# Raw features first for layer 0 of a bidirectional minGRU, with a late token scale and its chunks put between fusion tiles

## The chip, the cores and the metric

One NeuronCore of a Trainium2 chip runs the whole program. The metric is the device time of one execution in microseconds (us). TensorE is called PE, its weight loads PEld, VectorE DVE, ScalarE ACT, GpSimd POOL, SyncE SP.

## The reference

The input x is 8 batches of 512 tokens with 512 features. It is normalised per token, goes through four gated recurrent layers once forward and once backward in time with the same weights, both directions are joined by a linear layer ("fusion") and added to x. A feed-forward part with ternary weights follows; the change does not touch it.

```python
def mingru(x, W, b):                       # Wz = Wh = W, bz = bh = b in this case
    z  = sigmoid(x @ W.T + b)
    ht = tanh(x @ W.T + b)
    a  = clip(1.0 - z, 1e-8, 1 - 1e-8)
    return linear_scan(a, z * ht)          # h[t] = a[t]*h[t-1] + z[t]*ht[t]
def stack(x):
    h = x
    for i in range(4):
        h_new = mingru(h, W[i], b[i]) + (h if i > 0 else 0)
        h = layernorm(h_new, gamma, beta)  # per token, over 512 features
    return h
xn  = (x - mean(x)) / sqrt(var(x) + 1e-5)  # per token, without gamma and beta
x   = x + concat(stack(xn), flip(stack(flip(xn)))) @ fusion_W.T + fusion_b
out = x + ffn(layernorm_plain(x))          # absmean ternary weights, gelu, layernorm
```

## The kernel before

Everything is fp32. A **state** is one batch in one direction, kept features first: a tile `h` of 4 chunks of 128 features by 512 tokens (pool `h`, 6 buffers). Batches go in four pairs. Layers 1 to 3 run over the four states of a pair; layer 0 gives both directions of a batch from one set of gates, because it has the same input for both.

**The order is written out by hand** (`manual_schedule`). Its unit is a **slot** (function `slot`): some main work, and shares taken from queues. The main work of a layer is one **gate** chunk (`gates`, L378): four matmuls, which PE records as 8 passes, into a PSUM tile `u` (pool `ps_u`, 3 buffers), three activations on ACT (the factors a, z, t, L385 to L387), on DVE the clamp of a (L390) and the product z = z*t (L391), then the time scan (L400) and the residual add. Layer 0 does two scans for a chunk, one for each direction.

After a layer its state is normalised by going to tokens and back. **T** (`tokens` on `turned`, L272): four transposes into a PSUM tile `pt` (pool `ps_t`, 3 buffers), on DVE the statistics (`bn_stats` L137, `bn_aggr`, add of eps L141), POOL's power L144 for 1/sqrt, on DVE the bias `nmr` (L259), and ACT writes the normalised token tile (L263). **B** (`back`, L281): four transposes of the four token tiles into `pf`, and ACT copies them to `h` with gamma and beta (L287). Each state has four T and four B; `turns` and `backs` queue them, a slot takes one of each, or two of each where it is called with caps of 2. The last layer needs only 1/sqrt of the variance for each token (`norm_last`), which scales the output of fusion, and its residual adds come as four in a row (L433). `need` runs slots without main work until a state is ready: an **empty slot**. `Tokens` lets a B start one slot after the last T; at most `TOK` = 12 token tiles are held at once.

**x** of a later pair is normalised in layer 3 of the pair before, by the queues `xturns` and `xbacks`: tokens are loaded (`xn`), statistics and token tile as in T but without transposes, then B as `pf_x` into `xT` (`norm_x`). For the first two batches `start_x` does it ahead of all slots.

**Fusion** (`fusion`) has four tiles a batch, of 128 tokens each: on DVE the bias `fb` is added to the loaded x row `xf` (L449), PE makes 8 passes for each direction into a tile `pu` of its own (L454, from `ps_u` as well), DVE scales each by its 1/sqrt and adds it to the row (L464), which frees the `pu`; the row is stored. Between pairs four stages follow each other: layer 0 of batch b+2, fusion of b, layer 0 of b+3, fusion of b+1. In the fusion weights `fw` gamma, beta and the mean over features are folded once: `fold_beta` (16 passes, L530, and 8 scalings by gamma on DVE) and `fold_mean` for each direction (8 passes, L547, and 4 corrections on DVE).

Two side tasks ride on every second or fourth slot (`extra`): sums of absolute ternary weights in the first pair and their quantisation in the later ones, each loaded through the pool `stg` of 4 buffers. In the last pair the first feed-forward input is normalised as well (`norm_y`). All loads but the very first go through SP's queue.

Of the kernel before, what the change touches and what calls it, by code (L numbers as in the profile page):

```python
# [24 lines left out]
def kernel(  # L25
    ctx: ExitStack,
    tc: tile.TileContext,
    x: bass.AP,
    gru_wT: bass.AP,
# [19 lines left out]

    nc = tc.nc  # L50
# [8 lines left out]
    TOK = 12  # L59
# [9 lines left out]
    zp = ctx.enter_context(tc.tile_pool(name="z", bufs=16))  # L69
# [5 lines left out]
    stgp = rec.enter_context(tc.tile_pool(name="stg", bufs=4))  # L75
# [15 lines left out]
    def load_x(use, b, t, queue):  # L91
        xs[use, b, t] = xsp.tile([P, H], F32, tag="xs", name=f"x{use}_{b}_{t}")
        queue.dma_start(out=xs[use, b, t], in_=x[b, ts(t, P), :])

    def load_gw(l, queue):
        queue.dma_start(out=gw[l], in_=gru_wT[l].rearrange("(c p) h -> p c h", p=P))
# [8 lines left out]

    warm = const.tile([P, 1], F32, name="warm")
    nc.vector.memset(warm, 0.0)
    for t in range(0, NT, 2):
        load_x("n", 0, t, nc.sync)
        load_x("n", 0, t + 1, nc.scalar)  # L110
    load_gw(0, nc.scalar)
    nc.sync.dma_start(out=gb, in_=gru_b)
    for t in range(NT):
        load_x("n", 1, t, nc.sync)
# [5 lines left out]
    for l in range(1, L):  # L120
        load_gw(l, nc.sync)
# [66 lines left out]
    ctx.enter_context(tc.manual_schedule())  # L188
    with rec:
        gp = rec.enter_context(tc.tile_pool(name="gate", bufs=3))  # L190
        ps_u = rec.enter_context(tc.tile_pool(name="ps_u", bufs=3, space=PSUM))
        ps_t = rec.enter_context(tc.tile_pool(name="ps_t", bufs=3, space=PSUM))
# [6 lines left out]
        xT = {}  # L199
# [5 lines left out]
        class Tokens(list):  # L205


            def append(self, tile_):
                super().append(tile_)
                self.at = now[0] + 1  # L210
# [6 lines left out]
        def shares(cap_t, cap_b):  # L217


            mid, last = [], []  # L220
            for q, cap in ((turns, cap_t), (backs, cap_b)):
                for _ in range(cap):
                    if not q or not ready(q[0][0]):
                        break
                    take(q, mid, last)
            return mid, last

# [40 lines left out]
        def turned(zs, t, name):  # L268
            def source():
                pt = ps_t.tile([P, H], F32, tag="pt", name=f"pt_{name}")  # L270
                for c in range(NC_):
                    nc.tensor.transpose(pt[:, ts(c, P)], zs[c][:, ts(t, P)], ident)  # L272
                return pt
# [22 lines left out]
        def norm(s, zs, tag):  # L296
# [8 lines left out]
            for t in range(NT):  # L305
                queue(turns, s, at + 2, tokens(turned(zs, t, f"{tag}_{t}"), toks, None, f"{tag}_{t}"))
# [9 lines left out]
        def norm_x(b, at, gap):  # L316
            toks = Tokens()

            def dst():
                if b not in xT:  # L320
                    xT[b] = hp.tile([P, NC_, S], F32, tag="h", name=f"xT_{b}")
                return xT[b]

            for t in range(NT):
                queue(xturns, b, at + gap * t, tokens(lambda t=t: xs["n", b, t], toks, None, f"x{b}_{t}"))
            for c in range(NC_):
                queue(xbacks, b, toks, back(toks, dst, c, False, f"x{b}_{c}"))

        def norm_y(b):
            toks = Tokens()  # L330

# [25 lines left out]

        def slot(work=None, cap_t=1, cap_b=1):
            end = work() if work is not None else None
            mid, last = shares(cap_t, cap_b)  # L360
            m, e = x_shares()
            if end is not None:
                end(mid + m)
            else:
                for f in mid + m:
                    f()
# [6 lines left out]
        def gates(h, l, o, name, scans):  # L373

            def work():
# [7 lines left out]
                t = gp.tile([P, S], F32, tag="t", name=f"t_{name}")  # L383
                a = gp.tile([P, S], F32, tag="a", name=f"a_{name}")
                nc.scalar.activation(a, u, AF.Sigmoid, bias=ngb[:, l, o : o + 1], scale=-1.0)  # L385
                nc.scalar.activation(z, u, AF.Sigmoid, bias=gb[:, l, o : o + 1])  # L386
                nc.scalar.activation(t, u, AF.Tanh, bias=gb[:, l, o : o + 1])  # L387

                def end(mid):
                    nc.vector.tensor_scalar(a, a, CLAMP_HI, CLAMP_LO, ALU.min, ALU.max)  # L390
                    nc.vector.tensor_tensor(z, z, t, ALU.mult)  # L391
# [5 lines left out]

        def scan(dst, a, z, backward):
# [3 lines left out]
        def first_layer(b, cap=1):  # L402

            need(b)
            zf, zb = [], []
            h = xT[b]
            for o in range(NC_):
                def scans(a, z, o=o):
                    f = zp.tile([P, S], F32, tag="z", name=f"zf_{b}_{o}")
                    scan(f, a, z, False)  # L410
                    scan(z, a, z, True)
                    zf.append(f)
                    zb.append(z)
                slot(gates(h, 0, o, f"{b}_0_{o}", scans), cap, cap)
            state[b, 0] = xT.pop(b)
            now[0] -= 1
            norm((b, 0), zf, f"{b}0_0")
            norm((b, 1), zb, f"{b}1_0")
            now[0] += 1

        def layer(s, l, cap=1):
            need(s)
            zs = []
            h = state[s]
            for o in range(NC_):
                def scans(a, z, o=o):
# [4 lines left out]
                    elif o == NC_ - 1:  # L431
                        for c in range(NC_):
# [9 lines left out]
        def fusion(b):  # L442
            need((b, 0), (b, 1))
            hs = [state.pop((b, 0)), state.pop((b, 1))]
            rs = [rsv.pop((b, 0)), rsv.pop((b, 1))]
            for t in range(NT):
                def work(t=t):
                    xt = xs["f", b, t]
                    nc.vector.tensor_tensor(xt, xt, fb, ALU.add)  # L449
# [10 lines left out]
                    def end(mid):  # L460
                        for f in mid:
                            f()
                        for d in range(2):
                            nc.vector.scalar_tensor_tensor(  # L464
                                xt, pus[d], rs[d][:, t : t + 1], xt, ALU.mult, ALU.add
                            )
                        nc.sync.dma_start(out=x1[b][t], in_=xt)
                    return end
                slot(work, 2, 2)
# [56 lines left out]
        def fold_beta():  # L526
            pb = ps_u.tile([P, H], F32, tag="u", name="pb")
            for k in range(2 * NC_):
                c = k % NC_
                nc.tensor.matmul(  # L530
                    pb, lhsT=bet[:, c : c + 1].broadcast_to([P, P]), rhs=fw[:, k, :],
                    start=(k == 0), stop=(k == 2 * NC_ - 1),
                )

            def end(mid):
                for f in mid:
                    f()
                nc.vector.tensor_tensor(fb, pb, fb, ALU.add)
                for k in range(2 * NC_):
                    c = k % NC_  # L540
                    nc.vector.tensor_scalar(fw[:, k, :], fw[:, k, :], gam[:, c : c + 1], None, ALU.mult)
            return end

        def fold_mean(d):
            pm = ps_u.tile([P, H], F32, tag="u", name=f"pm_{d}")
            for c in range(NC_):
                nc.tensor.matmul(  # L547
                    pm, lhsT=ones, rhs=fw[:, d * NC_ + c, :], start=(c == 0), stop=(c == NC_ - 1),
                )

            def end(mid):
                for f in mid:
                    f()
                for c in range(NC_):
                    w = fw[:, d * NC_ + c, :]
                    nc.vector.scalar_tensor_tensor(w, pm, -1.0 / H, w, ALU.mult, ALU.add)
# [3 lines left out]
        def load_pair(use, b):  # L560
            for t in range(NT):
                load_x(use, b, t, nc.sync)

        def start_x(b):

            srcs = [xs["n", b, t] for t in range(NT)]
            found = [stats([s], f"x{b}_{t}") for t, s in enumerate(srcs)]
            toks = Tokens()
            for t in range(NT):
# [296 lines left out]
```

## Time and profile before

| what | value |
|---|---|
| median of 3 runs | 1796.99 us (1794.94 to 1797.65) |
| the profiled execution | 1797.87 us, of it span 1796.1 us |
| granted PE clock, mean | 0.994 |
| PE busy | 1727.9 us (96%) |
| DVE busy | 1438.8 us (80%) |
| ACT busy | 1025.8 us (57%) |
| POOL busy | 201.9 us (11%) |
| DMA | 83.33 MB, mean 46 GB/s |

Busy is the time in which an engine works on an instruction; passes of PE are pipelined, so their sum is more than the distance from start to start, which is used for prices. The span runs from the first to the last instruction of the profiled execution. Names such as L378 are lines of the kernel before.

### The profile page before, as it was taken

Reading aid. Unit: us, or ns where it says so; the run is one execution under the profiler, and the core shown is the slowest. Engines: PE = TensorE matmul, PEld = TensorE weight load, DVE = VectorE, ACT = ScalarE, POOL = GpSimd, SP = SyncE. Lnnn points to the kernel's source line nnn. Section 1 sums busy time; section 2 is a strip of 40 time slices with the busy share of each in tenths; the row PEclk is TensorE's granted clock in tenths of the full one; section 3 lists DMA queues with packets and bytes.
Section 4 is the critical chain, followed back from the end, with each engine's and each line's share of the span. In section 5 each row is a group of like instructions: output and inputs, shape, how many; then the busy total and the mean of one; then the engine's idle time right before and its main releaser. Section 6 shows DMA issues by size and latency. Waiting matters only on the chain.

```text
span 1796.1 us, 19346 instructions
## 1 busy us (share of the span) xinstructions
PE 1727.9 (96%) x6520; PEld 1052.0 (59%) x6520; DVE 1438.8 (80%) x2863; ACT 1025.8 (57%) x1664; POOL 201.9 (11%) x334
## 2 busy tenths in 40 slices
PE   5999999999999999999999999999999999999998
PEld 2555554444555444555544455554488888888886
DVE  5888989658998966999897699988368787768776
ACT  4677776337776522677752367773055656565563
POOL 1111112100111110111111011111000000000000
PEclk9999999999999999999999999999999999999999
DMA  6002111110110121111011121001301011101100
GB/s 217 7 24 63 49 31 46 47 46 1 48 59 24 47 70 36 36 60 52 31 47 65 41 83 53 1 24 53 127 32 48 10 38 47 48 1 47 48 24 24
DMA packets 42132, 83.33 MB, mean 46 GB/s; under 512 B 5040, under 2 KB 5040, under 8 KB 41008
## 3 DMA queue, kind: packets, MB, share of 16 engines
q1 hardware_dynamic: 41216, 80.52, 13.1%
q10 hardware_dynamic: 816, 1.57, 0.3%
q8 instruction: 51, 0.84, 0.2%
q14 instruction: 49, 0.40, 0.1%
HBM read 56.91 MB, written 25.17 MB: 46 GB/s over the span
## 4 chain that ended last, share of the span: by engine, by line
PE 59%; DVE 21%; ACT 12%; issue 5%; DMA 2%; POOL 1%; DVEq 0%; SPq 0%; POOLq 0%; ACTq 0%
PE u L378 20%; PE ph L690 11%; PE po L717 11%; PE pu L454 9%; DVE z L391 4%; DVE z L400 4%; DVE st L137 3%; PE pt L272 3%; ACT tok L263 3%; PE pf L281 2%; ACT t L387 2%; ACT z L386 2%; ACT a L385 2%; ACT xT L287 1%; DVE a L390 1%
## 5 line engine op out<-in xcount | busy, mean ns | idle before, releaser
L378 PE MATMUL u<-xT,gw 128*128 128x512 f32 x1024 | 461.0, 593 | 1.6 <-ACT xT L287 1.6
L378 PE MATMUL u<-h,gw 128*128 128x512 f32 x768 | 350.2, 599 | 0.0
L263 ACT ACTIVATE tok<-pt,nmr,rs 128x512 f32<-128x512 f32 x192 | 148.3, 777 | 324.8 <-DVE nmr L259 297.6
L378 PEld LDWEIGHTS u<-xT,gw 128*128 128x128 f32 x1024 | 185.4, 191 | 186.1 <-issue 182.4
L400 DVE TENSOR_TENSOR_SCAN z<-a,z 128x512 f32<-128x512 f32 x224 | 274.0, 1223 | 2.6
L137 DVE BATCH_NORM_STATS2 st<-pt 128x6 f32<-128x512 f32 x256 | 176.6, 690 | 85.9 <-PE pt L272 85.4
L378 PEld LDWEIGHTS u<-h,gw 128*128 128x128 f32 x768 | 140.9, 193 | 140.8 <-issue 140.8
L385 ACT ACTIVATE a<-u,ngb 128x512 f32<-128x512 f32 x224 | 153.3, 684 | 107.3 <-PE u L378 104.7
L694 ACT ACTIVATE g<-ph 128x512 f32<-128x512 f32 x128 | 76.2, 595 | 229.0 <-PE ph L690 229.0
L144 POOL TENSOR_TENSOR rs<-ve,mhalf 128x1 f32<-128x1 f32 x192 | 112.7, 587 | 814.5 <-DVE ve L141 670.2
L717 PE MATMUL po<-pwq,ghi 128*128 128x512 f32 x512 | 203.5, 397 | 0.0
L690 PE MATMUL ph<-yhi,fcq 128*128 128x512 f32 x512 | 199.7, 390 | 0.0
L717 PE MATMUL po<-pwq,glo 128*128 128x512 f32 x512 | 199.6, 390 | 0.0
L690 PE MATMUL ph<-ylo,fcq 128*128 128x512 f32 x512 | 199.4, 389 | 0.0
L391 DVE TENSOR_TENSOR z<-z,t 128x512 f32<-128x512 f32 x224 | 154.2, 689 | 27.3 <-ACT t L387 24.8
L387 ACT ACTIVATE t<-u,gb 128x512 f32<-128x512 f32 x224 | 155.6, 694 | 0.0
L386 ACT ACTIVATE z<-u,gb 128x512 f32<-128x512 f32 x224 | 153.7, 686 | 0.0
L705 DVE TENSOR_TENSOR acc<-acc,g 128x512 f32<-128x512 f32 x112 | 77.2, 689 | 92.9 <-ACT g L694 91.9
L281 PE MATMUL pf<-ident,tok 128*128 128x128 f32 x768 | 116.6, 275 | 12.4 <-ACT tok L263 9.2
L454 PE MATMUL pu<-fw,h 128*128 128x512 f32 x256 | 119.9, 612 | 8.5 <-DVE xf L464 8.4
L272 PEld LDWEIGHTS pt<-ident,z 128*128 128x128 f32 x640 | 79.3, 141 | 79.4 <-issue 71.4
L454 PE MATMUL pu<-fw,xT 128*128 128x512 f32 x256 | 115.1, 592 | 0.0
(127 smaller groups left out, 2291.5 us busy)
## 6 DMA issues: line engine op xcount, KB each, us to landing
xf<-in_x_dram SPq DMA_DIRECT2D x32, 256.0 KB, 3.8
x<-xf SPq DMA_DIRECT2D x32, 256.0 KB, 2.0
xy<-x SPq DMA_DIRECT2D x32, 256.0 KB, 4.3
out_dram<-xy SPq DMA_DIRECT2D x32, 256.0 KB, 2.1
xn<-in_x_dram SPq DMA_DIRECT2D x30, 256.0 KB, 4.5
fca<-in_fc_wT_dram SPq DMA_DIRECT2D x16, 256.0 KB, 2.9
pwa<-in_proj_wT_dram SPq DMA_DIRECT2D x16, 256.0 KB, 2.7
fcb<-in_fc_wT_dram SPq DMA_DIRECT2D x16, 256.0 KB, 3.5
```

The costliest lines, as they stand in the source:

```text
L137: nc.vector.bn_stats(st[:, i, :], p)
L263: nc.scalar.activation(tile_, src, AF.Identity, bias=nmr, scale=r)
L281: nc.tensor.transpose(pf[:, ts(t, P)], toks[t][:, ts(c, P)], ident)
L378: nc.tensor.matmul(u, lhsT=gw[l][:, c, ts(o, P)], rhs=h[:, c, :], start=(c == 0), stop=(c == NC_ - 1),)
L385: nc.scalar.activation(a, u, AF.Sigmoid, bias=ngb[:, l, o : o + 1], scale=-1.0)
L386: nc.scalar.activation(z, u, AF.Sigmoid, bias=gb[:, l, o : o + 1])
L387: nc.scalar.activation(t, u, AF.Tanh, bias=gb[:, l, o : o + 1])
L391: nc.vector.tensor_tensor(z, z, t, ALU.mult)
L400: nc.vector.tensor_tensor_scan(dst[:, d], a[:, d], z[:, d], 0.0, ALU.mult, ALU.add)
L454: nc.tensor.matmul(pu, lhsT=hs[d][:, c, ts(t, P)], rhs=fw[:, d * NC_ + c, :], start=(c == 0), stop=(c == NC_ - 1),)
L690: nc.tensor.matmul(ph, lhsT=w, rhs=ys[b][c][i], start=(c == 0 and i == 0), stop=(c == NC_ - 1 and i == 1),)
L717: nc.tensor.matmul(po[b][t], lhsT=part[:, ts(t, P)], rhs=pwq[k // NP_][:, k % NP_, :], start=(k == 0 and i == 0), stop=(k == NF - 1 and i ...
```

## The change

* The program gets x a second time, as `xt`, features first; the host lays it out, as it does the weights. A batch is loaded from it as `xT` (1 MB) by `load_xT`: both batches of the first pair at the start, each later one in layer 2 of the pair before.
* At the start the column mean of the first layer's weights `gw[0]` is taken out of them, so that gates on raw x equal gates on x minus its token mean. x in tokens is still loaded, for 1/sqrt of its variance alone (`norm_x`); `scale_x` spreads that over 128 partitions by four transposes of a broadcast column and ACT copies it to a tile `scale`. Token tiles and `pf_x` transposes of x are gone.
* A chunk of layer 0 has three stages, kept in `stages`: 8 PE passes; "factors", a given number of slots later: u times `scale` on DVE, then the three activations; "scans", one slot after that. `slot` runs what is due with `due`.
* Layer 0 chunks and fusion tiles alternate. `zlive` counts the z tiles in use, and a chunk waits in empty slots if two more don't fit in 16.
* The order of the activations becomes a, t, z. The pool `ps_u` has 4 buffers (was 3), `ps_t` 2 (was 3), `stg` 3 (was 4), `t` 2 (was 3); `TOK` is 10. `norm_y` starts its B two slots after the last T.
* Folding: `fold_sums` computes the sums with beta and with gamma together, in rows 0 and 64 of one product, kept in two token tiles until layer 1; `fold` picks the gamma row, divided by 512, and corrects and scales `fw` in one DVE step a chunk; `fold_bias` picks the beta row.
* The first loads alternate between SP and ACT in chunks of 256 KB.

The diff, cut; functions that go away whole are seen in the listing above.

```diff
-    TOK = 12
+    ZT = 16
+    TOK = 10
...
+    def load_xT(b):
+        xT[b] = hp.tile([P, NC_, S], F32, tag="h", name=f"xT_{b}")
+        nc.sync.dma_start(out=xT[b], in_=xt[b].rearrange("(c p) s -> p c s", p=P))
...
-    for t in range(0, NT, 2):
-        load_x("n", 0, t, nc.sync)
-        load_x("n", 0, t + 1, nc.scalar)
-    load_gw(0, nc.scalar)
+    xT[0] = hp.tile([P, NC_, S], F32, tag="h", name="xT_0")
+    for dst, part in ((gw[0], gru_wT[0]), (xT[0], xt[0])):
+        for c in range(NC_):
+            queue = nc.scalar if c % 2 else nc.sync
+            queue.dma_start(out=dst[:, c, :], in_=part[ts(c, P), :])
+    for t in range(NT):
+        load_x("n", 0, t)
     nc.sync.dma_start(out=gb, in_=gru_b)
+    load_xT(1)
...
-        ps_u = rec.enter_context(tc.tile_pool(name="ps_u", bufs=3, space=PSUM))
-        ps_t = rec.enter_context(tc.tile_pool(name="ps_t", bufs=3, space=PSUM))
+        ps_u = rec.enter_context(tc.tile_pool(name="ps_u", bufs=4, space=PSUM))
+        ps_t = rec.enter_context(tc.tile_pool(name="ps_t", bufs=2, space=PSUM))
...
+        def scale_x(b):
+            def go():
+                pf = ps_f.tile([P, S], F32, tag="pf", name=f"pr_{b}")
+                for t in range(NT):
+                    nc.tensor.transpose(pf[:, ts(t, P)], rx[b][:, t : t + 1].broadcast_to([P, P]), ident)
+                def last():
+                    scale[b] = gp.tile([P, S], F32, tag="scale", bufs=2, name=f"scale_{b}")
+                    nc.scalar.copy(scale[b], pf)
+                return None, last
+            return go
+        def norm_x(b, at):
+            rx[b] = small.tile([P, NT], F32, tag="rsv", name=f"rx_{b}")
             for t in range(NT):
+                queue(xturns, ("x", b), at + t, tokens(lambda t=t: xs["n", b, t], None, rx[b][:, t : t + 1], f"x{b}_{t}"))
+            queue(xbacks, ("x", b), at + NT + 1, scale_x(b))
...
         def slot(work=None, cap_t=1, cap_b=1):
             end = work() if work is not None else None
+            due("factors")
             mid, last = shares(cap_t, cap_b)
             m, e = x_shares()
+            mid += m
+            late = [s for s in stages if s[0] <= now[0] and s[1] == "scans"]
+            if late or end is None:
+                for f in mid:
+                    f()
+                mid = []
+            due("scans")
             if end is not None:
-                end(mid + m)
+                end(mid)
...
+        def first_layer(b, lag=0):
...
+            def chunk(o):
+                def work():
+                    while zlive[0] + 2 > ZT:
+                        slot(None, 2, 2)
+                    zlive[0] += 2
...
+                    def scaled():
+                        z = zp.tile([P, S], F32, tag="z", name=f"z_{name}")
+                        nc.vector.tensor_tensor(z, u, scale[b], ALU.mult)
+                        a, t = factors(z, z, 0, o, name)
+                        def scans():
+                            product(a, z, t)
...
+                            scan(f, a, z, False)
+                            scan(z, a, z, True)
...
+                        stages.append((now[0] + 1, "scans", scans))
+                    stages.append((now[0] + lag, "factors", scaled))
+                return work
+            return [chunk(o) for o in range(NC_)]
         def layer(s, l, cap=1):
+            while s not in state or any(x[1] == "scans" for x in stages):
+                slot(None, 2, 2)
             need(s)
...
+        def fold_sums(d):
+            ps = ps_u.tile([P, H], F32, tag="u", name=f"pfold_{d}")
+            for c in range(NC_):
                 nc.tensor.matmul(
+                    ps, lhsT=both[:, c, :, :].rearrange("p i r -> p (i r)"), rhs=fw[:, d * NC_ + c, :],
...
+        def fold(d):
+            pm = ps_u.tile([P, H], F32, tag="u", name=f"pm_{d}")
+            nc.tensor.matmul(pm, lhsT=picks[1], rhs=folded[d], start=True, stop=True)
...
-                    nc.vector.scalar_tensor_tensor(w, pm, -1.0 / H, w, ALU.mult, ALU.add)
+                    nc.vector.scalar_tensor_tensor(w, w, gam[:, c : c + 1], pm, ALU.mult, ALU.subtract)
...
+        pm0 = ps_u.tile([P, H], F32, tag="u", name="pm0")
+        for c in range(NC_):
+            nc.tensor.matmul(pm0, lhsT=ones, rhs=gw[0][:, c, :], start=(c == 0), stop=(c == NC_ - 1))
+        for c in range(NC_):
+            w = gw[0][:, c, :]
+            nc.vector.scalar_tensor_tensor(w, pm0, -1.0 / H, w, ALU.mult, ALU.add)
+        for b in range(2):
+            norm_x(b, 0)
...
+        f0, f1 = first_layer(0, NC_ - 1), first_layer(1, 2)
+        for work in f0:
+            slot(work, 2, 2)
...
+        slot(f1[0], 2, 2)
+        slot(f1[1], 2, 2)
+        slot(lambda: fold_sums(0), 2, 2)
+        slot(f1[2], 2, 2)
+        slot(f1[3], 2, 2)
+        slot(lambda: fold_sums(1), 2, 2)
...
+            for i in range(2):
+                load_pair("f", b + i)
+                firsts = first_layer(b + 2 + i) if not last_pair else [None] * NT
+                for first, tile_ in zip(firsts, fusion(b + i)):
+                    if first is not None:
+                        slot(first)
+                    slot(tile_, 2, 2)
```

## The prediction, made before the result was known

> **What bounds the kernel now.** I read the busy table first, then the chain that ended last, then a table by stage, then the timeline of TensorE (PE) with its gaps, then VectorE (DVE) beside it.
>
> ```profile
> PE 1727.9 (96%) x6520; PEld 1052.0 (59%) x6520; DVE 1438.8 (80%) x2863; ACT 1025.8 (57%) x1664; POOL 201.9 (11%) x334
> ...
> PE 59%; DVE 21%; ACT 12%; issue 5%; DMA 2%; POOL 1%; DVEq 0%; SPq 0%; POOLq 0%; ACTq 0%
> ```
>
> PE carries the end, but 21% of the chain is DVE: somewhere PE waits for it. The stages (from:to and length in us; then busy us of PE, PEld, DVE, ACT, POOL; clock; DMA share; GB/s) say where:
>
> ```profile
> 0.00:24.76 24.76, 4.07 (x16) 3.13 (x17) 8.97 (x34) 5.47 (x8) 4.75 (x14) 1.00 0.95 316
> 24.76:68.49 43.73, 41.91 (x145) 21.92 (x145) 34.97 (x62) 24.80 (x40) 3.79 (x7) 1.00 0.12 44
> 299.30:415.58 116.28, 111.30 (x362) 55.95 (x361) 77.11 (x152) 47.95 (x84) 12.35 (x22) 1.00 0.11 37
> 415.58:620.00 204.42, 199.10 (x715) 106.51 (x714) 192.17 (x401) 139.57 (x221) 30.84 (x51) 0.98 0.12 39
> 1297.00:1796.00 499.00, 490.94 (x2246) 405.66 (x2244) 368.64 (x667) 285.02 (x471) 27.23 (x36) 1.00 0.10 35
> ```
>
> The first 24.76 us are DMA-bound (share 0.95). Layers 1 to 3 of a pair (415 to 620) hold PE 97% and DVE 94%: both nearly full. The stretch from layer 0 to the last fusion tile (299 to 416, a **transition**) leaves DVE a third idle. The feed-forward part after 1297 is not touched. On PE's timeline in layer 3 (start, length, last bracket: idle before it):
>
> ```profile
> 556.37 0.60 PE L281 MATMUL pf<-ident,tok 128*128 128x128 f32 x4
> 559.31 0.55 PE L281 MATMUL pf_x<-ident,tok_x 128*128 128x128 f32 x3 [2.34 <-ACT xT L287]
> 560.18 5.29 PE L378 MATMUL u<-h,gw 128*128 128x512 f32 x8
> 565.75 0.60 PE L281 MATMUL pf<-ident,tok 128*128 128x128 f32 x4
> 566.18 0.60 PE L281 MATMUL pf_x<-ident,tok_x 128*128 128x128 f32 x4
> 566.62 3.60 PE L378 MATMUL u<-h,gw 128*128 128x512 f32 x8
> 570.05 0.60 PE L272 MATMUL pt<-ident,xT 128*128 128x128 f32 x4
> ```
>
> and in the transitions:
>
> ```profile
> 360.52 0.33 PE L281 MATMUL pf<-ident,tok 128*128 128x128 f32 x1 [2.65 <-ACT tok L263]
> ...
> 658.58 5.40 PE L454 MATMUL pu<-fw,h 128*128 128x512 f32 x8 [2.19 <-DVE xf L464]
> ...
> 711.06 5.40 PE L454 MATMUL pu<-fw,h 128*128 128x512 f32 x8 [2.15 <-DVE xf L464]
> ```
>
> Starts give the prices: a gate (8 passes) 570.05 - 566.62 = 3.43 us, four transposes 566.62 - 566.18 = 0.44. A steady slot (gate, four transposes "T" to tokens, four "B" back) is 4.31. Gaps of PE add up to about 60 us: 20 at the start, 8.6 in the first transition with the layer 3 ahead of it, 10.2 in the second, 10.0 in the third, 2.9 in the last pair, the rest early.
>
> [...] after the waits of 2.34, 2.50, 2.19, 2.15 us (second transition) and 2.50 (third) a group of eight passes took 4.7 to 5.4 us, not 3.60, so about 1.7 lost each, five times; after 2.65 (first) and 2.34 (at 879) none. [...] the row of L391 reads 689, and starts follow every 0.62, so the new multiply by the scale costs 0.62 of DVE. [...]
>
> **The change, part by part.** The sum is against the profiled execution, 1797.87 us (span 1796.1 and 1.8 around it), 0.9 above the median of 1796.99.
>
> *x features first.* Per row of x 16 transposes (L281 pf_x) become 4 for the scale. In layer 3 of three pairs: 6 rows x 12 x 0.109 = **-7.9 us** of PE. With them go 24 token writes (0.80) and as many copies (0.59) on ACT, which had room, and the bias products (0.15) on DVE. The six loads of 1 MB go through SP a layer ahead (landing 8.6 us, DMA share there 0.1 to 0.2): nothing, at worst a late load, which would show as SP waiting; nothing else queues behind them that is due within 10 us.
>
> *The stall in layer 3 stays.* At 555.93 the last T of a state is transposed, but DVE is 5.2 us behind (its statistics start at 561.23): x statistics (1.01 a slot) and the four adds of L433 (2.47) make a slot row of 20 to 21 us of DVE against 17.2 of PE. Without pf_x the next PE wait is the B in the slot after, for the token of that T: statistics to 562.2, product and bias to 563.1, token to 563.9, against PE ready at 560.7: 3 us. So 2.3 turns into 3 (2 in the first pair). The second stall (598.90, for tok_x) has no successor there, because the scale needs no tokens; DVE's lag of 6 us is carried into the transition.
>
> *Layer 0 between fusion tiles.* A chunk on DVE is 3.45 (clamp 0.33, product 0.67, scans 2.45) and now 4.07. Before, four chunks came in a row (4.45 with a statistic, against 3.87 of PE) and the tiles after them found DVE late: PE waited for a `pu` that L464 had not freed (the L464 waits). After, chunk and tile alternate: PE 10.3 bare, 11.6 with three T; DVE 6.5 to 10.9. With a fourth u buffer the L464 waits go. Two things replace them. The carried lag meets two token buffers in PSUM instead of three: the second T of the first tile waits about 2 us in pairs 1 and 2. And the order of PE shows, once in each transition, an **empty slot** in front of layer 1 of the fourth state: T, B, then T T B with no gate. Counting from the end t of the gate before: its z factor at t+2.0, product 2.65, token 3.6, so the second of the T T goes at 3.7 instead of 1.3 (2.4 us idle); its statistics end at 6.7, POOL and bias 7.4, two tokens 8.3, the copy to h 9.1, which the gate's fourth chunk needs, where PE is ready at 7.2 (2 us idle). **4.4 us**, three times.
>
> *Sum of stalls*, with half-clock time (1.7 for six in ten of those over 2 us): first transition 7 (was 8.6), second 12.5 (was 10.2 and four slow spells, 17), third 12.5 (was 11.7), last pair 1.5 (was 2.9; the y transposes come a slot later): **-6.5 us**. Bounds: every spell and 1 us more a stall, +5; empty slot half as long and no spells, -17.
>
> *Folding.* 16 L530 and 16 L547 passes become 16 for the sums, 4 and 4: 8 x 0.43 = 3.4 less, the scaling of fw (8 x 0.41 DVE) gone; the four corrections per direction stay on DVE, which is the longer side of that slot. **-2.5** (0 to -3.4).
>
> *The start.* 2.1 MB at about 345 GB/s (316 x 24.76 / 22.7, from 2 us on): gw by 6, x by 8.5. [...] four corrections of gw (0.65 each) feed the first gate at 10.7 instead of 24.76. Statistics of x (4.1 on DVE, POOL 0.6) lie under the three gates. PE reaches the scale's transposes at 21.1; with the copy (0.59) DVE's first multiply is at 22.3, where the first clamp was at 29.25. From there DVE is the chain: 8 chunks 27.6, 8 multiplies 5.0, 8 token statistics 8.1, one of x, two fills 0.7, biases 0.8; four waits for POOL of 0.66, because the bias now directly follows its statistics, and about 1.5 for T held by two token buffers: 47 us. Then two tokens, two copies, half a gate: the first layer 1 gate ends at 22.3 + 50.2 = 72.5, before at 73.8. **-1.5** (+2 if the clock stays low or loads are late, -6 if the held T are hidden).
>
> Edits at nothing: stage buffers 4 to 3 (SP's loads, landing 3 us, have two to four slots), TOK 12 to 10 (skips T of the last pair; its slot T T B B is in the 1.5), order of the activations (the product needs both).
>
> Sum: -7.9 - 6.5 - 2.5 - 1.5 = **-18.4**, so 1779.5 for the profiled execution, about **1779** for the median. Own range 1770 to 1789.
>
> **Rivals.** (1) *The lag is absorbed*: the fourth u buffer and DVE's spare third swallow the waits, no spells, 10 us more off: 1768. For it: DVE idle in 299 to 416. Against: the empty slot is a fixed chain. (2) *DVE becomes the bound* between tiles, ending slower: with two token buffers the three T of a chunk and tile wait for tokens behind scans; DVE 10.9 against PE 11.6 leaves 0.7 us, and a quantised piece (1.2) takes it. If two tiles a transition stall 2.5 us and drop to half clock (2.5 + 1.7 = 4.2 each), that is 6 x 4.2 = 25 on top: 1804. It decides once DVE's chain per pair of chunk and tile is above 11.6 + 18.4 / 24 = 12.4 us, with 24 such pairs in the three transitions. Against it: only three of eight chunk-tile pairs carry T T. (3) *Start and empty slots eat the gain*: start +4, empty slots 7 each, all spells: 1795, no change.
>
> **Numbers.** Likeliest 0.52, rival (1) 0.18, (2) 0.20, (3) 0.10; the first two are faster, the last is no change. About 0.2% (3.6 us) is what a measurement here can tell. Faster 0.52 + 0.18 = 0.70, same 0.10, slower 0.20. The range reaches from under rival (1)'s value to (2)'s: 1764 to 1804.
>
> **Right or wrong in the profile after.** First gate near 11 and first multiply near 22; no L464 waits over 1 us; three PE gap pairs of about 2.4 and 2 us before layer 1 of the fourth state; PE busy 10 us less. It is wrong if DVE's share of the chain rises well above 21%, if the waits in tiles are for tokens, or if the first layer 1 gate ends after 77.

## The result, and the profile after: slower, by a wait that stands

The changed kernel took 1824.14 us (median of 4, 1820.4 to 1827.5), the kernel before beside it 1797.32: a ratio of 1.0148, 95% interval 1.0123 to 1.0173. The forecast was 1779 with a range of 1764 to 1804 and 0.70 for faster. It is wrong in sign and out of range. The profile below is of the slowest of the four executions, 1827.5 us. Lines of the changed kernel are new ones: L417 is the gate of layers 1 to 3 (before L378), L463 that of layer 0, L305 the copy of B to h (L287), L279 the token write of T (L263), L290 the transposes of T (L272), L299 those of B (L281), L528 and L538 the two halves of a fusion tile (L454, L464).

The busy table and the chain of the page:

```profile
PE 1735.5 (95%) x6424; PEld 1049.3 (57%) x6424; DVE 1462.3 (80%) x2865; ACT 1008.3 (55%) x1612; POOL 203.7 (11%) x334
...
PE 61%; DVE 23%; ACT 8%; issue 5%; DMA 2%; POOL 0%; SPq 0%; DVEq 0%; POOLq 0%; ACTq 0%
```

PE issues 96 instructions fewer and yet is busy 7.6 us longer: its mean granted clock is lower (0.984, before 0.994; 0.984 to 0.988 over the four executions). Half clock stands here for spells in which the granted clock was near 0.5: 0.50 from 704.75 to 707.36 us, and 0.51 from 711.06 to 713.50 in the kernel before. The chain hardly differs. The groups of the page (out<-in, count, busy, mean, then idle time of PE just before them and who ended it) show what is new; the mean is of one pass, and eight pipelined passes take 3.60 us from the first start to the last end where nothing slows them:

```profile
L417 PE MATMUL u<-xT,gw 128*128 128x512 f32 x768 | 354.7, 603 | 15.2 <-ACT xT L305 15.2
L417 PE MATMUL u<-h,gw 128*128 128x512 f32 x768 | 352.4, 599 | 16.1 <-ACT h L305 16.1
```

In the page of before the same two rows are those of L378, layer 0 included:

```profile
L378 PE MATMUL u<-xT,gw 128*128 128x512 f32 x1024 | 461.0, 593 | 1.6 <-ACT xT L287 1.6
L378 PE MATMUL u<-h,gw 128*128 128x512 f32 x768 | 350.2, 599 | 0.0
```

So gates now wait **31.3 us** for the copies that B makes into their own input. The table by stage, in the columns used for before, says where:

```profile
12.23:67.31 55.08, 45.09 (x137) 24.23 (x137) 48.64 (x98) 24.75 (x38) 7.71 (x14) 0.89 0.42 149
67.31:300.41 233.10, 221.00 (x784) 116.75 (x783) 198.50 (x420) 162.60 (x280) 35.88 (x60) 0.97 0.15 48
300.41:391.35 90.94, 90.94 (x271) 44.16 (x269) 66.73 (x122) 31.79 (x54) 8.73 (x14) 1.00 0.15 50
391.35:612.95 221.60, 210.91 (x760) 112.53 (x759) 202.42 (x415) 147.39 (x228) 33.27 (x55) 0.98 0.15 48
612.95:720.51 107.56, 97.27 (x278) 47.25 (x277) 77.72 (x142) 26.96 (x40) 10.53 (x17) 0.95 0.17 54
720.51:950.25 229.74, 212.81 (x758) 112.83 (x757) 200.66 (x413) 147.36 (x228) 33.34 (x55) 0.98 0.15 49
950.25:1042.80 92.55, 92.04 (x278) 44.88 (x277) 72.48 (x137) 26.96 (x40) 10.53 (x17) 1.00 0.20 66
1042.80:1267.89 225.09, 209.56 (x762) 110.97 (x761) 196.21 (x397) 150.93 (x234) 30.73 (x51) 1.00 0.07 26
```

The layers of the four pairs in the kernel before:

```profile
68.49:297.98 229.49, 220.51 (x817) 118.46 (x815) 201.38 (x434) 169.06 (x290) 35.44 (x60) 1.00 0.14 43
396.69:613.45 216.76, 209.14 (x753) 111.85 (x752) 197.83 (x413) 149.29 (x238) 32.42 (x54) 0.98 0.12 39
718.04:932.93 214.89, 208.20 (x751) 110.84 (x750) 200.53 (x415) 147.32 (x234) 32.70 (x54) 0.99 0.14 44
1032.85:1240.21 207.36, 204.32 (x735) 108.62 (x733) 192.25 (x388) 144.19 (x226) 30.59 (x50) 1.00 0.10 35
```

| stage | before, us | after, us | difference |
|---|---|---|---|
| start and layer 0 of pair 0 | 68.5 | 67.3 | -1.2 |
| layers 1 to 3, pair 0 | 229.5 | 233.1 | +3.6 |
| first transition | 98.7 | 90.9 | -7.8 |
| layers, pair 1 | 216.8 | 221.6 | +4.8 |
| second transition | 104.6 | 107.6 | +3.0 |
| layers, pair 2 | 214.9 | 229.7 | +14.8 |
| third transition | 99.9 | 92.6 | -7.4 |
| layers, pair 3 | 207.4 | 225.1 | +17.7 |
| last fusion | 56.7 | 58.6 | +1.9 |

The feed-forward part is unchanged. The layers of pairs 1 to 3 lost 37.4 us. Of that 25.8 are time in which PE stands idle (length less busy time, 43.1 against 17.3); the other 11.6 are busy time, in part of transposes that moved here from the transitions. Pair 0 loses 3.6 us in another way: PE records 33 instructions fewer in its layers, but at a mean clock of 0.97 (before 1.00), and the stage ahead of them has 0.89 (before 1.00).

PE's timeline in the layers of pair 2 (start, length, last bracket the idle time before it):

```profile
782.87 1.12 PE L417 MATMUL u<-h,gw 128*128 128x512 f32 x2 [1.67 <-ACT h L305]
...
796.76 0.60 PE L290 MATMUL pt<-ident,z 128*128 128x128 f32 x4
797.19 0.60 PE L299 MATMUL pf<-ident,tok 128*128 128x128 f32 x4
797.63 2.74 PE L417 MATMUL u<-xT,gw 128*128 128x512 f32 x6
802.00 1.12 PE L417 MATMUL u<-xT,gw 128*128 128x512 f32 x2 [1.62 <-ACT xT L305]
```

A state starts every 19.1 us (782.87, 802.00), where four steady slots of 4.31 us are 17.2. The last B of the state (797.19) is transposed in the slot directly ahead of its own first gate; that gate runs six of its passes and waits for the fourth chunk. ACT's timeline at the same place shows what the copy waits for:

```profile
796.96 0.69 ACT L436 ACTIVATE a<-u,ngb 128x512 f32<-128x512 f32 x1
797.54 0.68 ACT L437 ACTIVATE t<-u,gb 128x512 f32<-128x512 f32 x1
798.11 0.69 ACT L438 ACTIVATE z<-u,gb 128x512 f32<-128x512 f32 x1
800.50 0.78 ACT L279 ACTIVATE tok<-pt,nmr,rs 128x512 f32<-128x512 f32 x1 [1.70 <-DVE nmr L275]
801.17 0.77 ACT L305 ACTIVATE xT<-pf,bet,gam 128x512 f32<-128x512 f32 x1
```

ACT is free at 798.8 and the transposed B is there, but the token write of the slot's T is ahead of the copy in ACT's order, and it waits until 800.50 for DVE's `nmr`. The gate can go on at 802.0.

### The profile page after: what moved, and what is told of

Same layout as the page of the kernel before. It is cut to its first block, busy times and chain, and to the rows that moved or that the text cites. A ratio compares the mean times of both kernels' runs of the same rounds, so it can differ in the third digit from the quotient of the medians.

```text
span 1825.5 us, 19093 instructions
## 1 busy us (share of the span) xinstructions
PE 1735.5 (95%) x6424; PEld 1049.3 (57%) x6424; DVE 1462.3 (80%) x2865; ACT 1008.3 (55%) x1612; POOL 203.7 (11%) x334
## 3 DMA queue, kind: packets, MB, share of 16 engines
q1 hardware_dynamic: 45776, 89.44, 14.5%
## 4 chain that ended last, share of the span: by engine, by line
PE 61%; DVE 23%; ACT 8%; issue 5%; DMA 2%; POOL 0%; SPq 0%; DVEq 0%; POOLq 0%; ACTq 0%
PE u L417 19%; PE ph L782 11%; PE po L809 11%; PE pu L528 9%; DVE z L447 4%; DVE z L443 4%; PE pt L290 4%; DVE st L151 4%; PE u L463 3%; ACT tok L279 3%; PE pf L299 2%; DVE a L442 2%; ACT xT L305 1%; DVE zf L447 1%; ACT z L438 1%
## 5 line engine op out<-in xcount | busy, mean ns | idle before, releaser
L417 PE MATMUL u<-xT,gw 128*128 128x512 f32 x768 | 354.7, 603 | 15.2 <-ACT xT L305 15.2
L417 PE MATMUL u<-h,gw 128*128 128x512 f32 x768 | 352.4, 599 | 16.1 <-ACT h L305 16.1
L279 ACT ACTIVATE tok<-pt,nmr,rs 128x512 f32<-128x512 f32 x192 | 148.4, 777 | 216.3 <-DVE nmr L275 202.6
L417 PEld LDWEIGHTS u<-xT,gw 128*128 128x128 f32 x768 | 139.6, 193 | 160.4 <-issue 131.1
L417 PEld LDWEIGHTS u<-h,gw 128*128 128x128 f32 x768 | 139.0, 192 | 159.7 <-issue 129.8
L436 ACT ACTIVATE a<-u,ngb 128x512 f32<-128x512 f32 x192 | 131.9, 687 | 119.6 <-PE u L417 112.9
L290 PEld LDWEIGHTS pt<-ident,z 128*128 128x128 f32 x640 | 80.6, 144 | 97.0 <-issue 58.0
L438 ACT ACTIVATE z<-u,gb 128x512 f32<-128x512 f32 x192 | 132.9, 692 | 0.0
L437 ACT ACTIVATE t<-u,gb 128x512 f32<-128x512 f32 x192 | 131.3, 684 | 0.0
L299 PE MATMUL pf<-ident,tok 128*128 128x128 f32 x768 | 119.5, 280 | 10.5 <-ACT tok L279 9.5
L436 ACT ACTIVATE a<-z,ngb 128x512 f32<-128x512 f32 x32 | 23.1, 721 | 175.7 <-DVE z L470 175.4
L528 PE MATMUL pu<-fw,h 128*128 128x512 f32 x256 | 115.3, 593 | 2.5 <-DVE xf L538 2.5
```

Of the source, the lines that this page charges most:

```text
L279: nc.scalar.activation(tile_, src, AF.Identity, bias=nmr, scale=r)
L299: nc.tensor.transpose(pf[:, ts(t, P)], toks[t][:, ts(c, P)], ident)
L417: nc.tensor.matmul(u, lhsT=gw[l][:, c, ts(o, P)], rhs=h[:, c, :], start=(c == 0), stop=(c == NC_ - 1),)
L528: nc.tensor.matmul(pu, lhsT=hs[d][:, c, ts(t, P)], rhs=fw[:, d * NC_ + c, :], start=(c == 0), stop=(c == NC_ - 1),)
```

## The experiments

**Theory S, the standing lag.** After a transition eight T of layer 0 are still to do. In the layers each slot takes one T and one B, each state brings four of each for its four slots: the queues are full and never recover. Before, layer 0 of the second batch ended four fusion tiles ahead of the layers, and the last B of a state came three slots ahead of its gate: counted on PE's order in pair 2, the last B that the first gate of layer 2 needs begins at 771.17 there and the gate at 785.01, with three other gates between; in the changed kernel these two begin at 797.19 and 797.63. **Rivals:** C, that the two pt buffers and the half-clock spells cost the time; D, that DVE is the bound and a wait removed comes back elsewhere.

**e1: copies ahead of token writes on ACT**, in the changed kernel.

```diff
+            split = 0
             for q, cap in ((turns, cap_t), (backs, cap_b)):
+                split = len(last)
...
-            return mid, last
+            return mid, last[split:] + last[:split]
```

> The changed kernel, with one order turned on ACT: in a slot the copies of B to h go ahead of the token writes of T. Theory S (standing lag: after a transition the queues of T and B run at their limit, so the last B of every state lies in the slot directly ahead of its first gate, and its copy on ACT stands behind a token write that waits for DVE): the waits of L417 for the copy, 31.3 us of PE in the changed kernel, fall under 5 us and the time falls by 28 to 38 us, to about 1790. Theory C (two pt buffers and the half-clock spells cost the time): the waits for token writes at pt stay or grow, the time falls by less than 12 us. Theory D (DVE is the bound, a wait that goes comes back elsewhere): within 5 us of 1824.

Measured: 1771.15 us, ratio to before 0.9864 (0.984 to 0.9887): 53 us less than the changed kernel, more than S's range. The waits of L417 are gone, as PE's waits of this kernel show (us in all, times, longest; this kernel's lines are two higher):

```profile
PE pt L292 <- ACT tok L281: 26.9, 10, 5.1
PE pf L301 <- ACT tok L281: 5.7, 5, 2.5
PE pm L655 <- DMA gw<-in_gru_wT_dram: 4.8, 1, 4.8
```

PE's waits add up to 45 us instead of 82, and its busy time falls from 1735.5 to 1713.2 with the same instructions. C and D are out as the main cause: the waits for pt are as before the edit (26.2 then) while the time fell, and the clock rose through the same edit (0.984 to 0.992). But not all of the 53 us is the standing lag. By stage, the layers of pairs 1 to 3 are 44.7 us shorter (209.4, 210.9 and 211.4), and those of pair 0 are 14.3 shorter (218.8), where no wait stands: the order on ACT cost time there too.

**e2: the queue cleared instead.**

```diff
-                    layer(s, l, 2 if s[0] == 0 and l == 1 else 1)
+                    layer(s, l, 2 if s[0] == b and l == 1 else 1)
```

> The changed kernel, with two T and two B allowed in each slot of layer 1 of the first two states of every pair (so far of the first pair alone), which clears the queue of layer 0. S: the empty slot goes, the last B of a state moves two or three slots ahead of its gate, the waits of L417 for copies go: 28 to 40 us less, 1784 to 1796. C: two T a slot with two pt buffers wait for tokens, the time stays at 1824 or rises. D: DVE has two statistics a slot for four slots, 3 to 5 us more of it per pair, the time within 8 us of 1824.

1793.27 us, 0.9979 (0.997 to 0.9988), 31 less than the changed kernel. With the order on ACT left as it was, taking the B off the slot ahead of its gate leaves 2.3 us of the 31.3. The 31 us are not all this wait: of 36 us between the two profiles the layers of pairs 1 to 3 have 15.6, the second transition 13.4 (94.1 us; see e9 and e11), and pair 0, which the edit leaves as it was, 4.9.

**e3: layer 0 in rows again.** Four chunks, then four tiles, all else as changed.

```diff
-                firsts = first_layer(b + 2 + i) if not last_pair else [None] * NT
-                for first, tile_ in zip(firsts, fusion(b + i)):
-                    if first is not None:
-                        slot(first)
-                    slot(tile_, 2, 2)
+                firsts = first_layer(b + 2 + i) if not last_pair else []
+                for first in firsts:
+                    slot(first)
+                for tile_ in fusion(b + i):
+                    slot(tile_, 2, 2)
```

> The changed kernel with the order of the kernel before in the transitions: four chunks of layer 0 in a row, then four fusion tiles; raw x, scale, stages, folding and pools as in the changed kernel. S: layer 0 is through four tiles ahead of layer 1, no empty slot, no waits for copies, but waits for pu in the tiles come back (two to five us per transition): 20 to 32 us less, 1792 to 1804. A rival, that alternating is good for the time and something else in the change is bad: each transition some 7 us longer, the layers as slow as now, 1835 to 1845.

1793.08 us, 0.9982 (0.9973 to 0.9991), again 31 less than the changed kernel. Gates wait 2.0 us for copies, the layers of pairs 1 to 3 are 38.4 us shorter and the transitions 9.7 longer. It is the alternating order that brings the lag, by ending layer 0 later; the rival with 1835 to 1845 falls.

**e4: the lag alone, in the kernel before.**

```diff
                 fusion(b)
-                first_layer(b + 3)
...
             fusion(b + 1)
+            if not last_pair:
+                first_layer(b + 3)
```

> The kernel before with one change: the second layer 0 of a transition comes after the second fusion instead of ahead of it. Nothing else of the change is in it. S: the empty slot and the standing lag appear here too, with waits of 0.8 to 1.7 us of the first gate of a state for its copy: 20 to 40 us slower than before, 1817 to 1837. C and D: the amount of work and the pools are as before, so within 8 us of 1797.

1842.11 us, 1.0259 (1.0236 to 1.0283), 45 us slower with no operation added, more than expected. PE's waits of this kernel:

```profile
PE u L378 <- ACT xT L287: 25.0, 16, 4.9
PE u L378 <- ACT h L287: 20.9, 14, 3.6
```

Gates wait 45.9 us for copies, where before had 1.6. It is the same signature without raw x, stages, pools or folding: S is shown from both sides.

**e5 and e6: copies first in the kernel before, and in e4.** The edit of e1.

> The kernel before with the copies of B ahead of the token writes of T on ACT, nothing else. S: the last B of a state lies some three slots ahead of its gate here, so the copies are not awaited and the order is worth little: of PE's waits those for copies (about 12 us in all, most ahead of transposes) may shrink and those for token writes grow, 1787 to 1800. A rival, that the order on ACT is good everywhere and has nothing to do with the standing lag: 20 us less or more, below 1780.

1774.93 us, 0.9888 (0.9873 to 0.9902). My expectation missed: 20 us, at the edge of the rival's. Before, PE waited 12.4 us for copies (1.6 for L378 and 10.8 for transposes that follow a copy), all of it goes, and the mean clock rises from 0.994 to 0.997. The layers of pair 0, which have no standing lag, are 8.7 us shorter (220.8 against 229.5). So a copy behind a token write costs PE in both orders of the slots; the standing lag makes it worse, it isn't the only place.

> The kernel before with the second layer 0 moved behind the second fusion, and with the copies ahead of the token writes. S: the waits of the first gates for their copies (46 us of PE with the late layer 0 alone) fall under 12, since a copy no longer stands behind a token write that waits for DVE; 1795 to 1812. If instead the queue's depth alone holds the gates up, the waits stay: 1830 to 1845.

1782.06 us, 0.9929 (0.9914 to 0.9944), 60 less than e4 and lower than expected; the waits of gates for copies fall from 45.9 to 5.0 us. The lag in the queues is still there and costs 7 against e5: it hurts through ACT's order.

**e7: both repairs in the changed kernel.**

> The changed kernel with both: copies ahead of token writes, and two T and two B a slot in layer 1 of the first two states of every pair. S: the two repair the same waits, so together they are worth little more than the copies first alone: the empty slots go (three times 2 to 4 us), two statistics a slot cost DVE something back; 1764 to 1776. If they repaired different waits, the gains would add (53 and 31): about 1740.

1765.35 us, 0.9833 (0.9819 to 0.9848). As S says, they mend the same waits; the gains do not add to 1740.

**e8: the pools.** The kernel of e1 with the pools of before.

```diff
-        ps_u = rec.enter_context(tc.tile_pool(name="ps_u", bufs=4, space=PSUM))
-        ps_t = rec.enter_context(tc.tile_pool(name="ps_t", bufs=2, space=PSUM))
+        ps_u = rec.enter_context(tc.tile_pool(name="ps_u", bufs=3, space=PSUM))
+        ps_t = rec.enter_context(tc.tile_pool(name="ps_t", bufs=3, space=PSUM))
```

> The changed kernel with copies ahead of token writes, and the pools of the kernel before: three buffers for pt, three for u and pu. Of PE's waits there 26.9 us are transposes of T that wait for a token write to free a pt. If the second pt buffer missing is their cause: these fall by half or more, those for pu rise from 2.6 to some 6 to 10, the time falls by 3 to 12 us, 1759 to 1768. If DVE's lag is the cause: the waits move to the B and the pu, and the time is within 4 us of 1771 or above.

1818.58 us, 1.0128 (1.0111 to 1.0145): 47 slower than e1. The first reading missed; the second had the direction (the waits move to `pu`, the time is not lower) and nothing of the size. PE's waits:

```profile
PE pu L530 <- DVE xf L540: 47.2, 17, 6.0
...
PE pt L292 <- ACT tok L281: 8.4, 3, 4.6
```

The pt waits do fall (26.9 to 8.4), but fusion tiles wait 47.2 us for u buffers (2.6 in e1): a raw chunk keeps its u until the multiply by the scale. In this order of slots the fourth u is worth more than the third pt. As both pools changed at once, the price of the second pt buffer by itself stays open, and with it the 26.9 us of pt waits.

**e9 and e11: the second transition.** It alone got longer. DVE's timeline there in the changed kernel, and SP's queue:

```profile
694.46 1.51 DVE L538 SCALAR_TENSOR_TENSOR xf<-pu,rsv,xf 128x512 f32<-128x512 f32 x2
700.03 0.48 DVE L166 TENSOR_SCALAR fcq<-fcb,lo_fc 128x512 f32<-128x512 f32 x1 [4.06 <-DMA fcb<-in_fc_wT_dram]
```

```profile
696.00 0.33 SPq L541 DMA_DIRECT2D x<-xf  x1
696.67 0.33 SPq L552 DMA_DIRECT2D fcb<-in_fc_wT_dram  x1
```

The load of a quantised piece (`fcb`) is queued on SP behind the store of the fusion tile, which waits for DVE's L538 (it ends at 695.97); DVE's next work is that piece, so it idles 4.06 us. PE then waits 4.64 us for a pt:

```profile
704.75 1.12 PE L290 MATMUL pt<-ident,z 128*128 128x128 f32 x4 [4.64 <-ACT tok L279]
707.36 5.13 PE L463 MATMUL u<-xT,gw 128*128 128x512 f32 x8
```

In e9 (the kernel of e7) and e11 (the changed kernel) no piece runs in that transition:

```diff
             for i in range(2):
                 load_pair("f", b + i)
+                if b == 2:
+                    pace[0] = 10**6
...
+            if b == 2:
+                pace[0] = 4
```

> The kernel of e7 (copies first, two T and two B a slot in layer 1 of the first two states) without quantised pieces in the transition from the second to the third pair: they wait until its layers begin. That transition alone is longer than before (107.6 against 104.6 us, the two others 7 shorter), with PE waits of 2.6 and 4.6 us ahead of T. Reading: a quantised piece's load is queued on SP behind the store of the fusion tile, which waits for DVE's L538, and DVE then waits 4.1 us for the load. If so, the transition falls to the 91 to 93 us of the two others, the time to some 1752 to 1761. If the second transition is long for another reason (x statistics carried over from layer 3), it stays over 100 us and the time at 1762 to 1768.

1763.31 us, 0.9815 (0.9801 to 0.9828). The transition took 90.9 us as expected, but the time is above the 1752 to 1761 that went with it and is not told apart from e7: there the transition was already 93.2, since the pieces fall on other slots. e11 has the edit in the changed kernel itself:

> The changed kernel with one edit: no quantised pieces in the second transition. In e7 this place was already short (93.2 us), so e9 did not separate it; here the order on ACT and the caps are those of the changed kernel, where the transition took 107.6 us and a piece's load was awaited 4.1 us by DVE. If pieces whose loads stand behind stores are what makes it long, it takes 91 to 95 us here, and the time falls by 8 to 16 us to 1808 to 1816, less whatever the pieces cost later. If not: the transition over 102 us, the time within 5 us of 1824.

1814.56 us, 1.0096 (1.0079 to 1.0113), 10 less than the changed kernel, and the transition took 94.2 us where it was 107.6: as expected, the pieces' place is the cause. That the load's wait behind the store is the part that matters is read from the lines above and not shown by e11, which takes the pieces' own work out of the transition too (DVE is busy 71.8 us in it instead of 77.7); e12 tests it elsewhere.

**e10: rows with copies first.** The edits of e1 and e3.

> The changed kernel with copies ahead of token writes, and layer 0 in rows of four chunks ahead of four fusion tiles, as before the change. Beside e1 (the same, with alternating) it gives the worth of alternating once the copies are not late, beside e5 (the kernel before with copies first) the worth of raw x, scale, folding and start, which the prediction put at 12 us. If alternating helps by itself, e10 is some 5 us slower than e1 (1776); if it only moves T and B into the layers, the same within 4 us (1767 to 1775) or faster.

1769.95 us, 0.9851 (0.9837 to 0.9864): not told apart from e1. Alternating is worth nothing by itself once the copies are not late. Of the 7.8 us that the first transition gained, PE's busy time has 5.1 (96.0 to 90.9) and its idle time 2.7: it records 39 instructions fewer there (271 against 310), all of them T and B, which moved into the layers behind. Against e5 it is 5 us lower, 0.4%, with intervals just apart, where the prediction had 12 for raw x, folding and start.

**e12: the loads of pieces ahead.** The kernel of e7.

```diff
+        early = {}
...
-            w = staged(part, i, f"{name}b")
+            w = early.pop((name, i), None)
+            if w is None:
+                w = staged(part, i, f"{name}b")
+            if i + 1 < NW:
+                early[name, i + 1] = staged(part, i + 1, f"{name}b")
```

> The kernel of e7 with the load of each quantised piece issued four slots early, when the piece before it runs. In e7 DVE waits 24.8 us for such loads, seven times. If those waits reach PE, 3 to 8 us less than e7: 1757 to 1763. If DVE has the room, the same within 3 us of 1765.

1759.36 us, 0.9788 (0.9773 to 0.9802), 6 less than e7, with an interval of its own, as expected; DVE no longer waits for these loads. The pieces still run in the second transition, and it takes 90.9 us with PE busy throughout (e7: 93.2). It is the fastest version here, 2.1% under the kernel before, with every part of the change in it. Most of that is not the change: the order on ACT alone gives the kernel before 1.1% (e5), and loads ahead were not tried there.

## Why the prediction was wrong, by its own steps

**The empty slot: the event right, its consequence missed. This is the step that failed.** It was priced at 4.4 us, as 2.4 ahead of T and 2 ahead of the gate. The profile has it, ahead of layer 1 of the third state and not of the fourth: 2.69 and 1.31 in pair 2, 2.69 and 1.83 in pair 3, 3.18 ahead of T in pair 1. But the sum took it as paid once in each transition. The prediction saw on PE's order that T T B came with no gate; it did not go on to ask what the queue looks like afterwards: one T and one B in every slot, none idle, so that the last B stays in the slot ahead of its gate. The wait returns at each state with 0.82 us in most of pairs 1 and 3 and 1.6 in pair 2. There DVE does a quantised piece just ahead of that slot's statistics (797.12 to 798.3 in the place shown); four slots a state and a piece every four slots put it in the same place each time. In pair 1 it falls a slot later. So L417's idle time comes to 31.3 us, of which 1.9 are in pair 0 (1.6 before). What the lag costs in all lies near 30 us: e2 and e3, which take it away and leave the order on ACT, gain 31 each, though 13.4 of e2's lie in the second transition. The 53 of e1 hold more, since that order costs some 20 us without the lag as well (e5). Between the profiles of the changed kernel and of e1 PE's gaps shrink by 37 us and its busy time by 22. From the mean clocks, 0.984 of 1825.5 us and 0.992 of 1766.8, the clock's part of the 22 is estimated at up to 15; it is rough, since the executions of the two kernels range over 0.984 to 0.988 and 0.989 to 0.993.

**"Sum of stalls" -6.5** was thus the mis-sized term (its own four entries add up to -6.7, and the slow groups of eight passes that it read as 4.7 to 5.4 us took 4.95 to 5.40): PE's gaps rose from 60 to 82 us (+22) instead. The half-clock time in the same term was set too low as well: the mean granted clock fell from 0.994 to 0.984, and PE's busy time, which was to fall by 10 us, rose by 7.6.

**The start -1.5** did not come. The first gate is at 12.2 (10.7 expected, which was the author's estimate; the eight passes of the column mean took 6.56 us and ended at 11.45), the first multiply at 23.9 (22.3). Layer 1 begins 1.2 us earlier than before, but its first gate, which the prediction counted to, is through at 75.1 (72.5 expected, 73.8 before): it stops 1.92 us for a copy, and its last four passes took 3.50 us at a granted clock of 0.55. That is 1.3 us later than before, inside the "+2 if the clock stays low" (the mean granted clock was 0.58 from 50 to 60 us). "About 1.5 for T held by two token buffers" is 9.9 us of PE waits there (5.00, 2.29, 2.60). A third buffer would have saved little of them: e8 has one and still waits 8.4 there, in a stage as long (55.1 us from the first gate on).

**"No L464 waits over 1 us":** nearly; 2.8 us are left of 8.4, the longest 1.4. The fourth u buffer does this, and much more than foreseen (e8).

**x features first -7.9 and folding -2.5:** the 96 instructions are gone and PE's waits for x tokens with them, but with copies first on both sides (e1 and e5) the change is 3.8 us at the medians, its interval overlapping. The idle time of the two is equal (45 us in each profile): the start wait and the waits for x tokens and `pu` gave way to 26.9 us for pt. PE's busy time is 7.0 us less.

**"Edits at nothing":** SP's loads were not nothing. The text allowed them "two to four slots", but a piece's load is issued in the slot in which DVE uses it, behind a store. DVE waits 23.2 us for these loads now, and had 14.5 us of such waits before. The pieces' place in the second transition cost 10 us (e11), and in e7 the late loads cost 6 (e12). This is the quantised piece of rival (2), in one transition of three, and by the lines shown through its load more than through DVE's busy time. The order of the three activations, `TOK`, the limit of 16 z tiles and the two queues of the first loads were not tried by themselves.

**The rivals.** None had the mechanism. The slower one, given 0.20, had the direction by luck: it put the loss in the tiles, yet PE's gaps in the first and third transitions are 0 and 0.5 us. Its sign, tiles in which PE waits for tokens, is seen in the second alone (2.55 and 4.64 us). The loss lies in layers 1 to 3, in code that the change doesn't touch.

## What to carry to other kernels

When a queue with a fixed rate feeds a loop with the same rate, a delay once put in stays: count the free slots of the queue after the event, and price a miss by the number of rounds until there are some. Where the copy that PE waited for stood behind a token write that waited 1.70 us for DVE, ACT did not begin it until 801.17, though free at 798.8: put the operation that the bottleneck waits for ahead of one that waits for another engine. Here two lines' order was worth 20 us in the old kernel and 53 in the new one. And a load issued where it is used can stand behind what its queue holds: the one issued at 696.67 came after a store that waited for DVE, and DVE then idled 4.06 us for it.

## What the runs showed of the hardware

Waits of PE of some 2 to 5 us are often, but not always, followed by slow passes. After the 4.64 us shown for the second transition eight passes took 5.13 us instead of 3.60, at a granted clock of 0.70. Of a first gate that began after 2.69 us in pair 2, six passes took 4.44 us at 0.62; in pair 3 the same gate, after the same wait, took the usual 2.74 at 1.00:

```profile
757.02 0.66 PE L290 MATMUL pt<-ident,z 128*128 128x128 f32 x4 [2.69 <-ACT tok L279]
757.95 4.44 PE L417 MATMUL u<-xT,gw 128*128 128x512 f32 x6
```

```profile
1079.86 0.65 PE L290 MATMUL pt<-ident,z 128*128 128x128 f32 x4 [2.69 <-ACT tok L279]
1080.79 2.74 PE L417 MATMUL u<-xT,gw 128*128 128x512 f32 x6
```

The kernel before is mixed in the same way: after the waits of 2.15 and 2.19 us that ended at 711.06 and 658.58 eight passes took 5.40 us, at a granted clock of 0.68; after those of 2.65, 2.31 and 2.34 us that ended at 360.52, 411.55 and 879.28 the next eight took 3.60, at 1.00. The short standing waits (0.82 to 1.83 us) leave the passes after them near their usual length (the last two passes of the gate in 1.12 or 1.13 us, at a granted clock of 1.00 after the 1.67 us at 782.87; 1.02 without a wait, at 419.46 in the kernel before), so there the loss is the idle time and little more. What decides between the two gates above was not found. So a wait of some 2 us or more can cost more than its idle time here, but how much a single one will cost can't be told from its length.
